# A selective scan whose input term for two of four states is made by ScalarE and TensorE: prediction and result

## The chip, the cores and the metric

The kernel runs on one core of a Trainium2 chip. A core has five engines with a queue of instructions each: TensorE (PE; its weight loads are listed apart as PEld), VectorE (DVE), ScalarE (ACT), GpSimd (POOL) and SyncE (SP), which here only starts DMAs. Each engine works through its queue in order; an instruction whose input or buffer isn't ready holds up all that stands behind it on the same engine. The metric is the device time of one launch in microseconds. The kernel before took 32,186.01 us (median of three runs, 32,183.83 to 32,190.26).

## The reference

Two layers on an image of 256 x 256 tokens with 128 channels, each with a group norm ahead and added to its input. Layer 0 is attention along rows. Layer 1, where the change lies, is a two-dimensional selective scan (four scan directions, 256 inner channels, 16 states per channel). Cut to what matters:

```python
delta = softplus(dts + dt_bias)                      # per token and channel
def step(h, inp):                                    # over 65,536 tokens
    d_t, x_t, B_t, C_t = inp
    dA = exp(d_t[..., None] * As)                    # channel x state
    h = dA * h + (d_t * x_t)[..., None] * B_t        # the input term is B * delta * x
    y = einsum('bkdn,bkn->bkd', h, C_t)              # sum over the 16 states
    return h, y
```

x_dbl = xs @ x_proj_w gives the 8 rows from which dts comes, and B and C of 16 rows each. The four directions' results are added, normalised, multiplied by a gate and projected.

## The kernel before, in words

The front part (both group norms, the attention, the input projection and the 3 x 3 convolution) ends at about 5,536 us of the profile and isn't touched. All the rest is the scan stage, from line 635 on.

**Tiling.** Each direction (order 2, 1, 3, 0) goes through 65,536 tokens in 128 chunks of T = 512 tokens: 512 chunks in all, numbered q. A chunk has NG = 8 steps g, one for each 32 of the 256 channels. A step has NI = 4 iterations n; each handles one state index i for all 32 channels, with four states j side by side: 4 x 32 = 128 partitions by 512 tokens. "Slot" means one such iteration, numbered 4g + n, 32 to a chunk. In a slot, in this order:

- ScalarE makes dA = exp(A * delta) from dr, the delta of 32 channels repeated over four states (line 1122). Some slots have an evacuation of sums (`evacuate`) here.
- One piece each of the generators that are due is emitted: `turn`, those in `later` (`store` or `finish` of a chunk that is done), `prepare`, and some of `products`.
- VectorE runs the scan h = dA * h + input along the 512 tokens (line 1148), with the last h of the chunk before from hst.

**The input term B * delta * x.** du = delta * x is made once per chunk. For three states i < NB = 3, TensorE spreads du over the four states into the PSUM tile ur (`spread_du`, line 864), and VectorE multiplies ur by B_r (`times_B`, line 875, 128 x 1536) into bx, in which the scans then run in place. For the fourth state, TensorE turns du to tokens x channels (`turn`, line 816), ScalarE copies it to duT (line 822) and multiplies by B, which is a number per token there (`products`, line 834: 32 ACTIVATEs of 128 x 128 per chunk), and TensorE turns the result back into the PSUM tile bl (`turn_back`, line 846, four transposes per step), from which the scan reads. One ur buffer and one bl buffer are there, three PSUM buffers for dA, two in SBUF for dAl (the dA of the fourth state), and two PSUM buffers "mm" that all other work shares.

**Behind the scans.** GpSimd copies the last h to hst (line 1167) and multiplies the four scanned states by C (line 1168). `sums` (line 890) adds up the states by TensorE products with a 0/1 matrix, 16 for each half of the channels: those of steps 0 to 3 are emitted at slots 23 and 24, those of steps 4 to 7 at slot 4 of the next chunk.

**Preparation of chunk q + 2** starts at slot 21 (g = 5, n = 1) with a piece per slot: transposes of the tokens (tps), copies to xs, the projection pb and its copy bc (line 747), the dt product pv, and then softplus as max(v, 0) + log1p(exp(-|v|)), with a correction of log1p's rounding: Abs, Relu, Exp, two Identity, Ln on ScalarE, and a subtraction and two additions on GpSimd. delta goes to memory and comes back spread (`spread_delta`, dr). `until(now, then)` is a row of empty pieces, which sets how many slots lie between two pieces.

**What sets the order.** `manual_schedule`: each engine gets its instructions in the order in which the Python code emits them. Buffers and data alone set the waits.

Of the kernel before, what the change touches and what calls it, by code (L numbers as in the profile page):

```python
# [16 lines left out]
P = 128  # L17
# [49 lines left out]
def attention_and_scan_kernel(  # L67
# [568 lines left out]
    NI = 4  # L636
    NB = 3
    sw = ctx.enter_context(tc.tile_pool(name="sw", bufs=1))
# [36 lines left out]
    for q in range(4):  # L675
# [3 lines left out]
        )  # L679
    neg_one = sw.tile([P, 1], F32, name="neg_one")  # L680
    nc.vector.memset(neg_one, -1.0)
    hst = sw.tile([P, NG, NI], F32, name="hst")
# [38 lines left out]
    def prepare(q):  # L721
# [5 lines left out]
        for h in range(2):  # L727
# [6 lines left out]
            yield  # L734
        yield from until(2, 5)
        for h, tp in enumerate(tps):
# [3 lines left out]
        for h in range(2):  # L740
            nc.tensor.matmul(  # L741
                pb, xw_in[:, k, h, :], xs[:, h, :], start=(h == 0), stop=(h == 1)
            )
        yield
        yield
        bc = io.tile([R + 2 * NS, T], F32, name="bc", bufs=1)
# [3 lines left out]
        yield  # L750


        e = io.tile([P, 2, T], F32, name="e", bufs=1)
# [21 lines left out]
        C_r = io.tile([P, NI, T], F32, name="C_r")  # L775
        for m, t, ni in ((0, B_r, NB), (1, C_r, NI)):
# [6 lines left out]
        yield  # L783
        lg = io.tile([P, 2, T], F32, name="lg", bufs=1)
        nc.scalar.activation(lg, e, AF.Identity, bias=1.0)
        yield
        du = io.tile([P, 2, T], F32, name="du")
        nc.scalar.activation(du, lg, AF.Identity, bias=neg_one)
        B_t = io.tile([P, 4, R + 2 * NS], F32, name="B_t")
        nc.scalar.copy(B_t, tp)  # L790
        yield
        nc.gpsimd.tensor_tensor(e, e, du, ALU.subtract)  # L792
        yield
        yield
        nc.scalar.activation(lg, lg, AF.Ln)  # L795
        yield
        nc.gpsimd.tensor_tensor(lg, lg, e, ALU.add)  # L797
        yield
        nc.gpsimd.tensor_tensor(delta, delta, lg, ALU.add)  # L799
        de_d = sd.tile([DI, T], F32, name="de_d")  # L800
        nc.sync.dma_start(de_d.rearrange("(h p) t -> p h t", p=P), delta)
        yield
        nc.gpsimd.tensor_tensor(du, delta, xs, ALU.mult)  # L803
        prepared[q] = xs, de_d, du, B_r, C_r, B_t

    def turn(q):

        duT = io.tile([P, 4, DI], F32, name="duT", bufs=1)
        turned[q] = duT
        tps = []  # L810
        for w in range(2):
            tp = sps.tile([P, 2, DI], F32, name="tpd", tag="mm")
            for b in range(2):
                for h in range(2):
                    t0 = (2 * w + b) * P
                    nc.tensor.transpose(
                        tp[:, b, h * P : (h + 1) * P], prepared[q][2][:, h, t0 : t0 + P], ident
                    )
            tps.append(tp)
        yield  # L820
        for w, tp in enumerate(tps):
            nc.scalar.copy(duT[:, 2 * w : 2 * w + 2, :], tp)
            yield

    def products(q, h):


        bt = wk.tile([P, 4, 4, 4, 32], F32, name=f"bt{h}", bufs=1)
        products_of[q, h] = bt
        duT, B_t = turned[q], prepared[q][5]  # L830
        for b in range(4):
            for j in range(4):
                n = R + NI * j + NB
                nc.scalar.mul(  # L834
                    bt[:, b, :, j, :],
                    duT[:, b, h * P : (h + 1) * P].rearrange("t (g c) -> t g c", c=32),
                    B_t[:, b, n : n + 1],
                )
                yield

    def turn_back(q, g):

        bl = sps.tile([P, T], F32, name="bl", bufs=1)
        bt = products_of[q, g // 4]
        for b in range(4):
# [4 lines left out]

    def spread_delta(q, h):

        de_d = prepared[q][1]
        dr = io.tile([P, 4, T], F32, name="dr")
        for j in range(4):
            nc.sync.dma_start(
                dr[32 * j : 32 * j + 32],
                de_d[h * P : (h + 1) * P, :].rearrange("(q c) t -> c q t", c=32),
            )
        return dr  # L860
# [86 lines left out]
    def finish(q, yos):  # L947
# [50 lines left out]
        for h in range(2):  # L998
# [86 lines left out]
    drain(preparing)  # L1085
    preparing.append(products(0, 0))
    drain(preparing)
# [3 lines left out]
    preparing.append(prepare(1))  # L1091
    for _ in range(2 * NI + 3):
        piece(preparing)
    begin_sums(0, 0)
    turning, multiplying, summing = [], [], []
    bls = {(0, 0): turn_back(0, 0)}
    multiplying.append(products(0, 1))
    for _ in range(4):
        piece(multiplying)


    counts = {1: [0, 0, 2, 2], 3: [2, 2, 2, 2], 5: [0, 0, 3, 3], 6: [2, 2, 2, 2], 7: [2, 2, 2, 0]}
    for s, (q, g) in enumerate(all_steps):
        k, a = steps[q]
        nxt = all_steps[s + 1] if s + 1 < len(all_steps) else None
        if g == 1:
            drs[q, 1] = spread_delta(q, 1)
# [4 lines left out]
        if g == 5 and q + 1 < NQ:  # L1112
            drain(preparing)
            drs[q + 1, 0] = spread_delta(q + 1, 0)
        dr = drs[q, g // 4][:, g % 4, :]
        hs = bxs.pop((q, g))
        for n, i in enumerate((NB, *range(NB))):
            if i < NB:
                dA = sps.tile([P, T], F32, name="dA", bufs=3)
            else:  # L1120
# [27 lines left out]
            nc.vector.tensor_tensor_scan(  # L1148
                hs[:, i, :],
                dA,  # L1150
                hs[:, i, :] if i < NB else bls.pop((q, g)),
                0.0 if a == 0 else hst[:, g, i : i + 1],
# [12 lines left out]
        if g % 4 == 3:  # L1165
            del drs[q, g // 4]
        nc.gpsimd.tensor_copy(hst[:, g, :], hs[:, :, T - 1])  # L1167
        nc.gpsimd.tensor_tensor(hs, hs, prepared[q][4], ALU.mult)  # L1168
        hcs[q, g] = hs
    drain([sums(NQ - 1, 1)])  # L1170
    summed[NQ - 1] = load_sum(NQ - 1)
# [62 lines left out]
```

## Time and profile before

| | |
|---|---|
| median of the runs | 32,186.01 us |
| the profiled execution, its span | 32,185.1 us |
| scan stage, from its first product at 5,576 us | 26,609 us |
| one chunk in directions 2, 1, 3 (distance of products at the same step) | 51.20 us |
| one chunk in direction 0, the last | 53.85 us (mean) |
| first product to last product of the four directions | 5,576 / 12,139 / 18,690 / 25,241 to 32,126 us |
| mean granted TensorE clock | 0.853 |

Busy times are unions over an engine's instructions. Two instructions in a row on one engine overlap at their ends, so the duration of one is longer than its share of the queue; the distance between the starts of two instructions that stand back to back is what one costs. In brackets behind an instruction of a timeline stands the idle time ahead of it, and what ended that.

### The profile page before, as it was taken

How to read it: one execution, taken by the hardware profiler on the slowest of the kernel's cores; microseconds unless marked ns; L12 is line 12 of the kernel's file. 1: busy time of each engine (PE TensorE's matmuls, PEld its weight loads, DVE VectorE, ACT ScalarE, POOL GpSimd, SP SyncE). 2: the span in 40 equal slices, each digit the busy share in tenths (PEclk: the TensorE clock that was granted, in tenths of full speed). 3: DMA queues.
4: the chain of work that ended last, by engine and by line, in shares of the span. 5: the costliest groups of instructions: out<-in, count | busy, mean ns of one | idle time of the engine just before them, and what ended most of it. 6: DMA issues, size and time to landing. Idle time of an engine off the chain costs nothing.

```text
span 32185.1 us, 380702 instructions
## 1 busy us (share of the span) xinstructions
PE 23853.4 (74%) x122902; PEld 10868.3 (34%) x122902; DVE 29575.2 (92%) x29023; ACT 25201.0 (78%) x50438; POOL 25710.4 (80%) x11291
## 2 busy tenths in 40 slices
PE   6999988666676667777777777777777777777777
PEld 3555544222222222222222232223222333333333
DVE  7666633999999999999999999999999999999999
ACT  5555522888888888888888888888888888888888
POOL 4222200999999999999999999999999999999998
PEclk9999999888888888888888888888888888888888
DMA  4001033444444444444444444444444555555554
GB/s 143 30 28 29 27 105 121 110 109 108 111 109 108 110 110 118 119 121 120 119 120 122 119 119 121 121 119 119 122 119 118 123 124 124 123 123 123 124 123 113
DMA packets 2100469, 3518.55 MB, mean 109 GB/s; under 512 B 201112, under 2 KB 1187096, under 8 KB 2022560
## 3 DMA queue, kind: packets, MB, share of 16 engines
q1 hardware_dynamic: 2093296, 3476.09, 43.3%
q8 instruction: 967, 15.84, 0.2%
q10 hardware_dynamic: 5168, 18.12, 0.1%
q14 instruction: 1038, 8.50, 0.1%
HBM read 2754.18 MB, written 739.25 MB: 109 GB/s over the span
## 4 chain that ended last, share of the span: by engine, by line
PE 32%; ACT 24%; DVE 22%; issue 12%; POOL 9%; DMA 2%; SPq 0%; ACTq 0%; POOLq 0%; DVEq 0%
DVE bx L1148 11%; PE yp L890 8%; DVE bx L875 7%; ACT dA L1122 6%; PE ur L864 6%; POOL bx L1168 5%; PE pb L741 3%; ACT bt L834 2%; PE pc L563 2%; ACT dAl L1122 2%; PE av L393 2%; PE tpy L913 2%; POOL at L370 2%; ACT e L765 2%; ACT L795 2%
## 5 line engine op out<-in xcount | busy, mean ns | idle before, releaser
L1168 POOL TENSOR_TENSOR bx<-bx,C_r 128x2048 f32<-128x2048 f32 x4096 | 18604.4, 4542 | 334.3 <-POOL hst L1167 5.8
L1148 DVE TENSOR_TENSOR_SCAN bx<-dA,hst,bx 128x512 f32<-128x512 f32 x12192 | 15074.4, 1264 | 217.2 <-ACT dA L1122 215.3
L1122 ACT ACTIVATE dA<-dr,A_s 128x512 f32<-128x512 f32 x12288 | 8329.3, 683 | 2247.5 <-DVE bx L1148 2199.6
L864 PE MATMUL ur<-du,spread 128*128 128x512 f32 x8192 | 5710.1, 787 | 4498.5 <-DVE bx L875 4378.8
L875 DVE TENSOR_TENSOR bx<-B_r,ur 128x1536 f32<-128x1536 f32 x4096 | 7075.5, 1727 | 40.1 <-DMA dr<-de_d 40.1
L834 ACT ACTIVATE bt<-duT,B_t 128x128 f32<-128x128 f32 x16384 | 5572.5, 392 | 698.7 <-PE bl L846 698.7
L1148 DVE TENSOR_TENSOR_SCAN bx<-dAl,hst,bl 128x512 f32<-128x512 f32 x4064 | 5096.6, 1254 | 24.2 <-PE bl L846 24.1
L890 PE MATMUL yp<-bx,gather 128*32 128x512 f32 x32768 | 5052.5, 771 | 7.5 <-POOL bx L1168 6.4
L846 PE MATMUL bl<-ident,bt 128*128 128x128 f32 x16384 | 2714.8, 289 | 2441.0 <-DVE bx L1148 2439.0
L846 PEld LDWEIGHTS bl<-ident,bt 128*128 128x128 f32 x16384 | 1791.0, 143 | 4323.4 <-DVE bx L1148 3240.7
L864 PEld LDWEIGHTS ur<-du,spread 128*128 128x128 f32 x8192 | 1451.2, 223 | 5027.9 <-DVE bx L875 5023.9
L370 POOL TENSOR_TENSOR at<-at,sm 128x2048 f32<-128x2048 f32 x256 | 922.2, 3603 | 2719.7 <-DVE sm L369 2550.6
L1122 ACT ACTIVATE dAl<-dr,A_s 128x512 f32<-128x512 f32 x4096 | 2919.2, 713 | 0.0
L890 PEld LDWEIGHTS yp<-bx,gather 128*32 128x32 f32 x32768 | 1165.1, 139 | 4348.3 <-issue 3834.9
L1167 POOL COPY hst<-bx 128x4 f32<-128x4 f32 x4096 | 771.4, 188 | 1615.5 <-DVE bx L1148 1588.6
L362 ACT ACTIVATE at<-at,mx 128x256 f32<-128x256 f32 x2048 | 1016.1, 498 | 472.5 <-DVE mx L358 468.1
L792 POOL TENSOR_TENSOR e<-e,du 128x1024 f32<-128x1024 f32 x512 | 1202.8, 2349 | 138.3 <-DMA C_r<-bc_d 138.3
L799 POOL TENSOR_TENSOR delta<-delta,lg 128x1024 f32<-128x1024 f32 x512 | 1209.9, 2363 | 40.1
L803 POOL TENSOR_TENSOR du<-delta,xs 128x1024 f32<-128x1024 f32 x512 | 1205.4, 2354 | 40.2
L758 PE MATMUL pv<-bc,dtw_s 8*128 8x512 f32 x2048 | 1019.6, 616 | 256.5 <-ACT bc L747 256.5
L797 POOL TENSOR_TENSOR lg<-lg,e 128x1024 f32<-128x1024 f32 x512 | 1205.0, 2354 | 0.2 <-ACT lg L795 0.2
L391 DVE COPY aT<-atp 128x512 f32<-128x512 f32 x512 | 353.6, 691 | 774.8 <-PE atp L382 771.0
(173 smaller groups left out, 31933.7 us busy)
## 6 DMA issues: line engine op xcount, KB each, us to landing
dr<-de_d SPq DMA_DIRECT2D x4096, 256.0 KB
C_r<-bc_d SPq DMA_DIRECT2D x2048, 256.0 KB
B_r<-bc_d SPq DMA_DIRECT2D x2048, 192.0 KB
de_d<-delta SPq DMA_DIRECT2D x512, 512.0 KB
xtok<-xc_d SPq DMA_DIRECT2D x256, 512.0 KB
xtok<-xc_d SPq DMA_DIRECT2D x512, 256.0 KB
yl<-y_d SPq DMA_DIRECT2D x512, 256.0 KB
y_d<-yt SPq DMA_DIRECT2D x512, 256.0 KB
```

Source lines behind the costliest of these rows:

```text
L370: nc.gpsimd.tensor_tensor(at, at, sm.unsqueeze(3).to_broadcast([P, H, 2, S]), ALU.mult,)
L797: nc.gpsimd.tensor_tensor(lg, lg, e, ALU.add)
L799: nc.gpsimd.tensor_tensor(delta, delta, lg, ALU.add)
L803: nc.gpsimd.tensor_tensor(du, delta, xs, ALU.mult)
L834: nc.scalar.mul(bt[:, b, :, j, :], duT[:, b, h * P : (h + 1) * P].rearrange("t (g c) -> t g c", c=32), B_t[:, b, n : n + 1],)
L846: nc.tensor.transpose(bl[:, b * P : (b + 1) * P], bt[:, b, g % 4].rearrange("t j c -> t (j c)"), ident)
L864: nc.tensor.matmul(ur, spread[:, g % 4].rearrange("p j c -> p (j c)"), prepared[q][2][:, g // 4, :], start=True, stop=True,)
L875: nc.vector.tensor_tensor(bx[:, :NB, :], prepared[q][3], ur.unsqueeze(1).to_broadcast([P, NB, T]), ALU.mult,)
L890: nc.tensor.matmul(yp[32 * g : 32 * g + 32, :], gather, hc[:, i, :], start=(i == 0 and steps[q][0] != ORDER[0]), stop=True, skip_group_che ...
L1122: nc.scalar.activation(dA, dr, AF.Exp, scale=A_s[:, k, g // 4, g % 4, i : i + 1])
L1148: nc.vector.tensor_tensor_scan(hs[:, i, :], dA, hs[:, i, :] if i < NB else bls.pop((q, g)), 0.0 if a == 0 else hst[:, g, i : i + 1], ALU.mult,
L1168: nc.gpsimd.tensor_tensor(hs, hs, prepared[q][4], ALU.mult)
```

## The change

NB goes from 3 to 2: the input term of two states, not one, is made on tokens by ScalarE and turned back by TensorE. So `times_B` covers 128 x 1024, `products` makes 64 multiplications per chunk (two tiles bt per half of the channels), and `turn_back` is called twice per step, with two bl buffers; the dA buffers in PSUM go from three to two. The order of states within a step alternates (2, 0, 3, 1). Softplus is one ScalarE function on the two halves of pv, and the arithmetic around it on ScalarE and GpSimd goes. dr is loaded for two steps at a time, two steps ahead. duT has two buffers. The loads of B_r and C_r stand under the last `until` of `prepare`, the four transposes of du ahead of each copy in `turn`, and in `products` each of the two tiles gets 16 multiplications with a piece each. The pieces of `prepare`, `turn` and `finish` are placed anew, and two `products` pieces are emitted in every slot.

```diff
-    NB = 3
+    NB = 2
+    SHARE = 0
-    neg_one = sw.tile([P, 1], F32, name="neg_one")
-    nc.vector.memset(neg_one, -1.0)
 def prepare(q):
-        yield from until(2, 5)
+        yield from until(2, 3)
         for h, tp in enumerate(tps):
             nc.scalar.copy(xs[:, h, ::-1] if k >= 2 else xs[:, h, :], tp)
             yield
...
-        yield
-        yield
+        yield from until(5, 7)
         bc = io.tile([R + 2 * NS, T], F32, name="bc", bufs=1)
         nc.scalar.copy(bc, pb)
...
+        yield from until(8, 10)
+        for h, pv in enumerate(pvs):
+            nc.scalar.activation(
+                delta[:, h, :], pv, AF.Softplus, bias=dtb_s[:, k, h : h + 1]
+            )
+        de_d = sd.tile([DI, T], F32, name="de_d")
+        nc.sync.dma_start(de_d.rearrange("(h p) t -> p h t", p=P), delta)
         yield
-        yield
-        for h, pv in enumerate(pvs):
-            nc.scalar.activation(e[:, h, :], pv, AF.Abs, bias=dtb_s[:, k, h : h + 1])
-            nc.scalar.activation(delta[:, h, :], pv, AF.Relu, bias=dtb_s[:, k, h : h + 1])
-            yield
         tp = sps.tile([P, 4, R + 2 * NS], F32, name="tpb", tag="mm")
...
-        nc.scalar.activation(e, e, AF.Exp, scale=-1.0)
+        yield from until(11, 13)
+        du = io.tile([P, 2, T], F32, name="du")
+        nc.gpsimd.tensor_tensor(du, delta, xs, ALU.mult)
+        B_t = io.tile([P, 4, R + 2 * NS], F32, name="B_t")
+        nc.scalar.copy(B_t, tp)
...
+        yield from until(13, 20)
         for m, t, ni in ((0, B_r, NB), (1, C_r, NI)):
...
-        nc.scalar.activation(lg, e, AF.Identity, bias=1.0)
-        nc.scalar.activation(du, lg, AF.Identity, bias=neg_one)
-        nc.gpsimd.tensor_tensor(e, e, du, ALU.subtract)
-        nc.scalar.activation(lg, lg, AF.Ln)
-        nc.gpsimd.tensor_tensor(lg, lg, e, ALU.add)
-        nc.gpsimd.tensor_tensor(delta, delta, lg, ALU.add)
 def turn(q):
-        duT = io.tile([P, 4, DI], F32, name="duT", bufs=1)
+        duT = io.tile([P, 4, DI], F32, name="duT")
         for w in range(2):
...
+            yield
+            nc.scalar.copy(duT[:, 2 * w : 2 * w + 2, :], tp)
 def products(q, h):
+        bts = [wk.tile([P, 4, 4, 4, 32], F32, name=f"bt{h}{i}", bufs=1) for i in range(NI - NB)]
+        for i, bt in enumerate(bts):
...
-def turn_back(q, g):
+def turn_back(q, g, i):
+        bl = sps.tile([P, T], F32, name=f"bl{i}", bufs=1)
-def spread_delta(q, h):
+def spread_delta(q, g):
-        dr = io.tile([P, 4, T], F32, name="dr")
+        dr = io.tile([P, 2, T], F32, name="dr")
 def finish(q, yos):
-        for j, now, then in ((0, 15, 16), (1, 16, 19), (2, 19, 20), (3, 20, 27)):
+        for j, now, then in ((0, 15, 16), (1, 16, 19), (2, 19, 20), (3, 20, 23)):
-        yield from until(27, 31)
+        yield from until(23, 25)
...
-        yield from until(33, 36)
+        yield from until(27, 28)
...
-        yield from until(36, 40)
+        yield from until(28, 30)
...
-        yield from until(40, 55)
+        yield from until(30, 39)
...
-        yield from until(55, 58)
+        yield from until(39, 41)
...
-    preparing.append(products(0, 0))
+    preparing.extend([products(0, 0), products(0, 1)])
-    counts = {1: [0, 0, 2, 2], 3: [2, 2, 2, 2], 5: [0, 0, 3, 3], 6: [2, 2, 2, 2], 7: [2, 2, 2, 0]}
+    PER = 2
+        if g % 2 == 0 and s + 2 < len(all_steps):
+            drs[all_steps[s + 2]] = spread_delta(*all_steps[s + 2])
-        for n, i in enumerate((NB, *range(NB))):
+        for n, i in enumerate((NB, 0, NB + 1, 1)):
             if i < NB:
-                dA = sps.tile([P, T], F32, name="dA", bufs=3)
+                dA = sps.tile([P, T], F32, name="dA", bufs=2)
-            if g == 4 and n == 3 and q + 1 < NQ:
+            if n == 3 and g == 1 and q + 1 < NQ:
                 turning.append(turn(q + 1))
-            if g == 5 and n == 2 and q + 1 < NQ:
+            if n == 0 and g == 3 and q + 1 < NQ:
                 multiplying.append(products(q + 1, 0))
-            if g == 7 and n == 1 and q + 1 < NQ:
+            if n == 0 and g == 7 and q + 1 < NQ:
                 multiplying.append(products(q + 1, 1))
             if g == 5 and n == 1 and q + 2 < NQ:
                 preparing.append(prepare(q + 2))
-            for _ in range(counts[g][n] if g in counts else 0):
+            for _ in range(PER):
                 piece(multiplying)
...
             if n == 1 and nxt:
                 bxs[nxt] = times_B(nxt[0], urs.pop(nxt))
-            if n == 3 and nxt:
-                bls[nxt] = turn_back(*nxt)
+            if n % 2 and nxt:
+                bls[(*nxt, n // 2)] = turn_back(*nxt, n // 2)
             if n == 3 and s + 2 < len(all_steps):
                 urs[all_steps[s + 2]] = spread_du(*all_steps[s + 2])
```

More of the change, by code (lines that the diff above doesn't have):

```diff
@@ L750, in prepare @@
         yield
-        e = io.tile([P, 2, T], F32, name="e", bufs=1)
         delta = io.tile([P, 2, T], F32, name="delta", bufs=1)
@@ L772, in prepare @@
             )
-        nc.scalar.activation(e, e, AF.Exp, scale=-1.0)
+        yield from until(11, 13)
[3 more added lines that the diff above has]
+        nc.scalar.copy(B_t, tp)
         B_r = io.tile([P, NB, T], F32, name="B_r")
         C_r = io.tile([P, NI, T], F32, name="C_r")
+        prepared[q] = xs, de_d, du, B_r, C_r, B_t
+        yield from until(13, 20)
         for m, t, ni in ((0, B_r, NB), (1, C_r, NI)):
@@ L782, in prepare @@
                 )
-        yield
-        lg = io.tile([P, 2, T], F32, name="lg", bufs=1)
-        nc.scalar.activation(lg, e, AF.Identity, bias=1.0)
-        yield
-        du = io.tile([P, 2, T], F32, name="du")
-        nc.scalar.activation(du, lg, AF.Identity, bias=neg_one)
-        B_t = io.tile([P, 4, R + 2 * NS], F32, name="B_t")
-        nc.scalar.copy(B_t, tp)
-        yield
-        nc.gpsimd.tensor_tensor(e, e, du, ALU.subtract)
[L793 to L796, printed above, removed]
-        nc.gpsimd.tensor_tensor(lg, lg, e, ALU.add)
-        yield
-        nc.gpsimd.tensor_tensor(delta, delta, lg, ALU.add)
[L800 to L804, printed above, removed]
     def turn(q):
-        duT = io.tile([P, 4, DI], F32, name="duT", bufs=1)
+        duT = io.tile([P, 4, DI], F32, name="duT")
         turned[q] = duT
-        tps = []
         for w in range(2):
@@ L818, in turn @@
                     )
-            tps.append(tp)
+            yield
+            nc.scalar.copy(duT[:, 2 * w : 2 * w + 2, :], tp)
         yield
-        for w, tp in enumerate(tps):
-            nc.scalar.copy(duT[:, 2 * w : 2 * w + 2, :], tp)
-            yield
     def products(q, h):
-        bt = wk.tile([P, 4, 4, 4, 32], F32, name=f"bt{h}", bufs=1)
-        products_of[q, h] = bt
+        bts = [wk.tile([P, 4, 4, 4, 32], F32, name=f"bt{h}{i}", bufs=1) for i in range(NI - NB)]
+        products_of[q, h] = bts
         duT, B_t = turned[q], prepared[q][5]
[L831 to L839, printed above, removed]
-    def turn_back(q, g):
-        bl = sps.tile([P, T], F32, name="bl", bufs=1)
-        bt = products_of[q, g // 4]
+        for i, bt in enumerate(bts):
+            for b in range(4):
+                for j in range(4):
+                    n = R + NI * j + NB + i
+                    to = bt[:, b, :, j, :]
+                    of = duT[:, b, h * P : (h + 1) * P].rearrange("t (g c) -> t g c", c=32)
+                    by = B_t[:, b, n : n + 1]
+                    if SHARE and (4 * b + j) % SHARE == SHARE - 1:
+                        nc.gpsimd.tensor_scalar(to, of, by, None, ALU.mult)
+                    else:
+                        nc.scalar.mul(to, of, by)
+                    yield
+    def turn_back(q, g, i):
+        bl = sps.tile([P, T], F32, name=f"bl{i}", bufs=1)
+        bt = products_of[q, g // 4][i]
         for b in range(4):
@@ L857, in spread_delta @@
                 dr[32 * j : 32 * j + 32],
-                de_d[h * P : (h + 1) * P, :].rearrange("(q c) t -> c q t", c=32),
+                de_d[32 * g : 32 * g + 64, :].rearrange("(q c) t -> c q t", c=32),
             )
@@ L1091, in attention_and_scan_kernel @@
     preparing.append(prepare(1))
-    for _ in range(2 * NI + 3):
-        piece(preparing)
+    drain(preparing)
     begin_sums(0, 0)
     turning, multiplying, summing = [], [], []
[L1096 to L1099, printed above, removed]
-    counts = {1: [0, 0, 2, 2], 3: [2, 2, 2, 2], 5: [0, 0, 3, 3], 6: [2, 2, 2, 2], 7: [2, 2, 2, 0]}
+    bls = {(0, 0, i): turn_back(0, 0, i) for i in range(NI - NB)}
+    PER = 2
     for s, (q, g) in enumerate(all_steps):
@@ L1105, in attention_and_scan_kernel @@
         nxt = all_steps[s + 1] if s + 1 < len(all_steps) else None
-        if g == 1:
-            drs[q, 1] = spread_delta(q, 1)
+        if g % 2 == 0 and s + 2 < len(all_steps):
+            drs[all_steps[s + 2]] = spread_delta(*all_steps[s + 2])
         if g == 2 and q and steps[q - 1][0] != ORDER[0]:
@@ L1111, in attention_and_scan_kernel @@
             load(q + 2)
[L1112 to L1115, printed above, removed]
+        dr = drs[q, g - g % 2][:, g % 2, :]
         hs = bxs.pop((q, g))
-        for n, i in enumerate((NB, *range(NB))):
+        for n, i in enumerate((NB, 0, NB + 1, 1)):
             if i < NB:
-                dA = sps.tile([P, T], F32, name="dA", bufs=3)
+                dA = sps.tile([P, T], F32, name="dA", bufs=2)
             else:
@@ L1150, in attention_and_scan_kernel @@
                 dA,
-                hs[:, i, :] if i < NB else bls.pop((q, g)),
+                hs[:, i, :] if i < NB else bls.pop((q, g, i - NB)),
                 0.0 if a == 0 else hst[:, g, i : i + 1],
@@ L1164, in attention_and_scan_kernel @@
                 piece(summing)
-        if g % 4 == 3:
-            del drs[q, g // 4]
         nc.gpsimd.tensor_copy(hst[:, g, :], hs[:, :, T - 1])
@@ L1169, in attention_and_scan_kernel @@
         hcs[q, g] = hs
+        if g % 2:
+            del drs[q, g - 1]
     drain([sums(NQ - 1, 1)])
```

## The prediction

> **What bounds the kernel now.** I read the page's busy shares and costliest groups first, then the busy time of one whole chunk, then the timelines of VectorE, ScalarE and TensorE in that chunk. A slot is one pass of the inner loop, numbered 4g + n within a chunk (32 slots, four to a step).
>
> ```profile
> PE 23853.4 (74%) x122902; PEld 10868.3 (34%) x122902; DVE 29575.2 (92%) x29023; ACT 25201.0 (78%) x50438; POOL 25710.4 (80%) x11291
> ...
> L875 DVE TENSOR_TENSOR bx<-B_r,ur 128x1536 f32<-128x1536 f32 x4096 | 7075.5, 1727 | 40.1 <-DMA dr<-de_d 40.1
> L834 ACT ACTIVATE bt<-duT,B_t 128x128 f32<-128x128 f32 x16384 | 5572.5, 392 | 698.7 <-PE bl L846 698.7
> ```
>
> ```profile
> 20005.40:20056.60 51.20, 36.27 (x160) 15.03 (x160) 50.99 (x41) 43.43 (x85) 46.85 (x20) 0.83 0.48 120
> ```
>
> The columns of the second line are window, length, busy PE, PEld, DVE, ACT, POOL, granted clock, DMA share, GB/s. In one chunk VectorE is busy 50.99 of 51.20 us: it is the bound. ScalarE has 7.8 us free, TensorE 14.9, GpSimd 4.4.
>
> ```profile
> 20011.06 1.73 DVE L875 TENSOR_TENSOR bx<-B_r,ur 128x1536 f32<-128x1536 f32 x1
> 20012.70 2.45 DVE L1148 TENSOR_TENSOR_SCAN bx<-dA,hst,bx 128x512 f32<-128x512 f32 x2
> 20015.07 1.25 DVE L1148 TENSOR_TENSOR_SCAN bx<-dAl,hst,bl 128x512 f32<-128x512 f32 x1
> 20016.24 1.26 DVE L1148 TENSOR_TENSOR_SCAN bx<-dA,hst,bx 128x512 f32<-128x512 f32 x1
> 20017.42 1.73 DVE L875 TENSOR_TENSOR bx<-B_r,ur 128x1536 f32<-128x1536 f32 x1
> ```
>
> Instructions overlap, so I cost by distance of starts: the product takes 1.64 us, a scan 1.18, a step 6.36.
>
> ```profile
> 20003.41 0.97 ACT L834 ACTIVATE bt<-duT,B_t 128x128 f32<-128x128 f32 x3
> 20004.29 0.71 ACT L1122 ACTIVATE dAl<-dr,A_s 128x512 f32<-128x512 f32 x1
> 20004.90 0.68 ACT L834 ACTIVATE bt<-duT,B_t 128x128 f32<-128x128 f32 x2
> ...
> 20017.33 0.58 ACT L747 COPY bc<-pb 40x512 f32<-40x512 f32 x1 [0.91 <-PE pb L741]
> ...
> 20031.22 1.28 ACT L795 ACT_TABLE_LOAD   x1
> 20032.52 1.06 ACT L795 ACTIVATE lg<-lg 128x1024 f32<-128x1024 f32 x1
> 20033.59 1.28 ACT L1122 ACT_TABLE_LOAD   x1
> ```
>
> A bt costs 0.295 us (0.88 for three), an Exp 0.61, a load 1.30. ScalarE already waits for TensorE at bc; that is harmless now because it runs ahead of VectorE.
>
> ```profile
> 20006.48 2.08 PE L864 MATMUL ur<-du,spread 128*128 128x512 f32 x2 [2.16 <-DVE bx L875]
> 20008.48 5.52 PE L890 MATMUL yp<-bx,gather 128*32 128x512 f32 x32
> 20013.93 0.66 PE L846 MATMUL bl<-ident,bt 128*128 128x128 f32 x4
> 20014.42 1.02 PE L864 MATMUL ur<-du,spread 128*128 128x512 f32 x2
> 20015.38 1.91 PE L741 MATMUL pb<-xs,xw_in 128*40 128x512 f32 x4
> ...
> 20025.56 1.70 PE L864 MATMUL ur<-du,spread 128*128 128x512 f32 x2 [2.16 <-DVE bx L875]
> 20027.19 4.70 PE L890 MATMUL yp<-bx,gather 128*32 128x512 f32 x32
> ```
>
> Twice a chunk 16 gather products (32 records) go to TensorE in one burst: 5.45 us or 4.64, by start distance. bl of step 7 comes out behind the first burst at 20013.93 + 0.66 = 20014.59, and its scan starts at 20015.07: 0.5 us to spare.
>
> **The sums, part by part.**
>
> VectorE: the product covers 1024 elements, not 1536. Two thirds of 1.64 us is 1.10; I take 1.11. Step 4 x 1.18 + 1.11 = 5.83, chunk 46.6 (now 50.9): 4.3 us less.
>
> ScalarE: 32 more bt x 0.295 = +9.4. Removed: Abs and Relu 4 x 0.57, Exp and Identity (128x1024) 0.95 each, Identity with a bias tile 1.04, Ln 1.07: -6.3. Softplus is in no row; its nearest is Abs on the same tile, 0.57 (between a copy's 0.48 and 0.67 for gz): two make 1.1. The two loads per chunk stay if Softplus, like Ln, isn't loaded together with Exp; the ends are no load (-2.7) and four (+2.6). I take two. Net +4.3, so ScalarE needs 43.4 + 4.3 = 47.7 us. Counted from starts alone: 32 x (0.61 + 0.59) = 38.5 and 8.4 for the rest = 46.9. It now needs as long as VectorE. Per slot it has 1.46 - 1.20 = 0.25 us to gain on it.
>
> The price per state shows in these rows: VectorE gives up 0.53 us a step, ScalarE takes four bt, 1.18 us, and TensorE four transposes, 0.49.
> [...]
>
> TensorE: 32 more transposes at about 0.165 = +5.2, 41.5 us. GpSimd: three of 2.35 us go, 46.9 - 7.1 = 39.8; du stays. Cover for both is the longer chunk.
>
> SP: 16 issues of dr per chunk, not 8 (0.46 us each, 1.85 for four), half as large; B_r and C_r move to slot 9 of the next chunk, behind dr, yl and xtok, about 3 MB in step 2. At the 209 GB/s that the busiest stretch of this chunk shows (share 1.02) that is 14.4 us, and dr for step 6 is issued 12 us after them and read 12 us after that: hidden. If not, ScalarE stands at step 6 for the rest. de_d goes out earlier, at slot 31, ahead of two chunks' slack. The prologue makes 48 more bt: +14 us. The two set-up instructions for neg_one are nothing.
>
> Order is where it costs. Two bl and one ur buffer: bl of state 2 is refilled in slot n = 1, that of state 3 at n = 3, ahead of ur. So TensorE in step 5 waits until scan 22 has read the second bl, 1.18 us later than now, and issues four transposes before ur and the burst. pb moves from slot 28 to 26, bc from 30 to 28.
>
> The dA buffers go from three to two, like dAl's: ScalarE can be four slots (5.8 us) ahead at most. duT's second buffer removes a wait that the trace doesn't list; nothing is counted for it.
>
> *Stretch A*, from the end of scan 22, with the cheaper burst (1.63 + 4.64) and handoffs of 0.05: transposes 0.05 to 0.55; ur to 2.18; burst to 6.82; bl for step 7 to 7.31, ready 7.48; pb 7.31 to 9.22. Scan 28 would start at 5 x 1.18 + 1.11 = 7.01: it waits to 7.5. ScalarE stands at bc until 9.27, though about 2 us ahead. Then bc 0.48, two bt 0.59, dA29 0.69: scan 29 starts at 11.05, not 8.19. Its lead is gone. dA30 starts 11.54, yo comes between, dA31 13.22; from 13.83 a load (1.44 with its wait), two Softplus 1.2, two bt 0.59, a load 1.30, so dA32 is ready at 19.1. Scan 32 would start at 12.84: 6.3 us lost.
>
> *Stretch B*, from the end of scan 2: the burst drained at slot 4 ends at 6.82, bl at 7.31; the first du transposes of turn are ready at 7.97. ScalarE, 2.0 us ahead by then (8 x 0.25), stands at duT until 8.02; copy 0.48, bt 0.59, dA9 0.69: scan 9 at 9.8, not 8.19: 1.6 lost. A further 0.2 goes at slot 12, where yo falls.
>
> Chunk: 46.6 + 6.3 + 1.6 + 0.2 = 54.7 us, now 51.2. With the dearer burst (ur 2.0, burst 5.45: 1.18 more in each stretch) 57.1. With TensorE at full clock throughout (ur 0.95, the burst eight rounds of 0.43 = 3.44, 1.88 less) A loses 4.4 and B nothing: 51.1. I take the cheaper burst, because TensorE will be somewhat busier ahead of it.
>
> The clock: matmuls of 512 columns take 0.59 us in the stretch with a granted clock of 1.00 and 1.06 where it is 0.51; both bursts begin slow behind 2.16 us of waiting. After the change 2.4 us of waiting for scan 22 remain ahead of the burst, so it begins slow again.
> [...]
>
> The last direction (128 chunks) has 1.57 us of VectorE statistics, two yn at slots 31 and 32 (0.49 each) and part of gz (2 x 0.67, less the lead of 0.85): +2.9, so 57.6. Moving finish closer gains nothing else; it lies beside the waits.
>
> Total: 5576 to the first product, 14, 384 x 54.7 = 21,005, 128 x 57.6 = 7,373, and 55 behind the last step: 34,023. The same sum for now, 5576 + 384 x 51.2 + 128 x 53.85 + 55 = 32,185, is the profiled execution's span of 32,185.1; the median of the runs shown is 32,186.0, so I carry nothing over. Predicted: 34,020.
>
> **Rivals.**
> 1. *Faster:* ScalarE never really waits for TensorE and both engines run near full. For it: neither's own sum passes 47.7. Against: pb and bl stand behind a burst in TensorE's order. It decides if the path from scan 22 to bc is under about 5.5 us instead of 9.3. Chunk 47.3, last direction 50.9: 5645 + 18,163 + 6,515 = 30,320.
> 2. *Level:* TensorE stays at full clock, chunk 51.1 and 54.0: 5645 + 19,622 + 6,912 = 32,180. Against: the idle time before the bursts.
> 3. *Dearer burst, or extra loads:* 57.1 and 60.0 give 35,250; four loads give 34,020 + 512 x 2.6 = 35,350.
> 4. *No load for Softplus:* 34,020 - 512 x 2.7 = 32,640. Against: Ln costs two.
>
> **How the numbers follow.** Likeliest 0.62 (33,400 to 35,000), rival 1 0.15, rival 2 0.08 (of it 0.03 faster, 0.03 same, 0.02 slower), rival 3 0.09, rival 4 0.06. A measurement tells about 0.2%, 64 us. Faster 0.18, same 0.03, slower 0.79. The range leaves out rival 1 and what lies above 35,300: 32,150 to 35,300, for the likeliest case alone 33,400 to 35,000.
>
> **What would show it.** VectorE under 0.90 busy in the scan, waiting for ScalarE's dA mostly; ScalarE waiting for pb at bc (some 2 to 5 us a chunk) and for tpd at duT; the wait for scans down from 2083 us; the product at about 1.2 us mean, x4096; two loads per chunk. I am wrong if bc finds pb ready, or if VectorE stays above 0.97 busy.

## The result and the profile after

The changed kernel takes 33,548.5 us (median of four runs, 33,523 to 33,571) against 32,184.9 us: a ratio of 1.0425, 95% interval 1.0412 to 1.0437. The forecast was 34,020 us. The profiled execution spans 33,558.9 us; the figures per chunk below come from distances between the products `times_B` in that trace. Where nothing else is said they are means: in the first three directions the distance from a direction's first product to the next direction's, over 128 chunks, in the last the mean distance of products at the same step. The directions run in the order 2, 1, 3, 0; 1 and 3 are called the middle ones.

The busy shares and the groups of the changed kernel's page, in the columns of before (line, engine, instruction, count, busy us, mean ns, idle before with its main releaser):

```profile
PE 25097.2 (75%) x139286; PEld 13094.5 (39%) x139286; DVE 27574.9 (82%) x29022; ACT 27076.5 (81%) x63747; POOL 22258.1 (66%) x9755
...
L819 ACT ACTIVATE bt<-duT,B_t 128x128 f32<-128x128 f32 x32768 | 11294.2, 396 | 4.3 <-PE bl L827 4.3
...
L856 DVE TENSOR_TENSOR bx<-B_r,ur 128x1024 f32<-128x1024 f32 x4096 | 4896.8, 1196 | 51.7 <-PE ur L845 48.3
...
L745 ACT COPY bc<-pb 40x512 f32<-40x512 f32 x512 | 297.8, 582 | 1959.1 <-PE pb L740 1959.1
L800 ACT COPY duT<-tpd 128x512 f32<-128x512 f32 x1024 | 598.9, 585 | 1268.9 <-PE tpd L796 1268.9
```

The product did become cheaper, 1,196 ns for 1,727: 2,179 us of busy time over 4,096 of them. And ScalarE now waits 1,959 us for pb and 1,269 us for the transposes of du; before, the trace had 455 us and 9 us for these two. VectorE went from 92% to 82% busy. No engine is busy for nine tenths of the time any more.

One chunk of direction 3 (window, length, busy PE, PEld, DVE, ACT, POOL, granted clock, DMA share, GB/s):

```profile
20002.90:20057.50 54.60, 39.27 (x192) 19.59 (x192) 47.12 (x41) 46.99 (x111) 40.10 (x18) 0.81 0.40 108
```

VectorE needs 47.1 us and ScalarE 47.0 us, in a chunk of 54.6. 7.5 us are waits of both. Stretch A of the prediction, from the end of scan 22 at about 20,002.9, on TensorE:

```profile
20002.97 1.08 PE L827 MATMUL bl<-ident,bt 128*128 128x128 f32 x4 [2.48 <-DVE bx L1122]
20003.85 1.91 PE L845 MATMUL ur<-du,spread 128*128 128x512 f32 x2
20005.69 3.94 PE L871 MATMUL yp<-bx,gather 128*32 128x512 f32 x32
20009.56 0.66 PE L827 MATMUL bl<-ident,bt 128*128 128x128 f32 x4
20010.15 1.91 PE L740 MATMUL pb<-xs,xw_in 128*40 128x512 f32 x4
```

on ScalarE:

```profile
20006.71 0.73 ACT L1096 ACTIVATE dAl<-dr,A_s 128x512 f32<-128x512 f32 x1
20012.10 0.58 ACT L745 COPY bc<-pb 40x512 f32<-40x512 f32 x1 [4.65 <-PE pb L740]
...
20016.74 1.28 ACT L759 ACT_TABLE_LOAD   x1
20018.03 1.26 ACT L759 ACTIVATE delta<-pv,dtb_s 128x512 f32<-128x512 f32 x2
...
20019.89 1.28 ACT L1096 ACT_TABLE_LOAD   x1
20021.19 0.72 ACT L1096 ACTIVATE dAl<-dr,A_s 128x512 f32<-128x512 f32 x1
```

and on VectorE:

```profile
20010.33 1.28 DVE L1122 TENSOR_TENSOR_SCAN bx<-dAl,hst,bl 128x512 f32<-128x512 f32 x1 [0.51 <-PE bl L827]
20013.88 1.28 DVE L1122 TENSOR_TENSOR_SCAN bx<-dA,hst,bx 128x512 f32<-128x512 f32 x1 [2.28 <-ACT dA L1096]
...
20021.94 1.28 DVE L1122 TENSOR_TENSOR_SCAN bx<-dAl,hst,bl 128x512 f32<-128x512 f32 x1 [3.30 <-ACT dAl L1096]
```

Read the three together. TensorE can't refill bl for step 6 before scan 22 has read it, so ur, the burst of sums, bl for step 7 and pb all come late. ScalarE has made dA28 and stands at bc for 4.65 us. Scan 28 waits 0.51 us for bl. Scan 29 waits 2.28 us for a dA that ScalarE could only begin behind bc. Then, with no lead left, the two loads and Softplus make scan 32 wait 3.30 us. Counted from 20,002.9, bc starts after 9.2 us, scan 29 after 11.0, scan 32 after 19.0.

### The profile page after: what moved, and what is told of

Its sections match the earlier page's. It is cut to its first block, busy times and chain, and to the rows that moved or that the text cites. A ratio compares the mean times of both kernels' runs of the same rounds, so it can differ in the third digit from the quotient of the medians.

```text
span 33558.9 us, 434075 instructions
## 1 busy us (share of the span) xinstructions
PE 25097.2 (75%) x139286; PEld 13094.5 (39%) x139286; DVE 27574.9 (82%) x29022; ACT 27076.5 (81%) x63747; POOL 22258.1 (66%) x9755
## 4 chain that ended last, share of the span: by engine, by line
ACT 37%; PE 32%; DVE 14%; issue 6%; DMA 6%; SPq 2%; POOL 2%; ACTq 0%; POOLq 0%; DVEq 0%
ACT bt L819 14%; PE yp L871 10%; DVE bx L1122 9%; ACT dA L1096 7%; ACT dAl L1096 6%; PE ur L845 4%; PE bl L827 4%; DMA B_r<-bc_d 3%; PE pb L740 3%; DVE bx L856 2%; ACT L1096 2%; PE pc L563 2%; ACT L759 2%; PE av L393 2%; POOL at L370 2%
## 5 line engine op out<-in xcount | busy, mean ns | idle before, releaser
L1122 DVE TENSOR_TENSOR_SCAN bx<-dAl,hst,bl 128x512 f32<-128x512 f32 x8128 | 10301.3, 1267 | 2206.3 <-ACT dAl L1096 1740.1
L827 PE MATMUL bl<-ident,bt 128*128 128x128 f32 x32768 | 6047.2, 315 | 7586.9 <-DVE bx L1122 7586.4
L1122 DVE TENSOR_TENSOR_SCAN bx<-dA,hst,bx 128x512 f32<-128x512 f32 x8128 | 10246.1, 1261 | 1361.2 <-ACT dA L1096 1361.2
L819 ACT ACTIVATE bt<-duT,B_t 128x128 f32<-128x128 f32 x32768 | 11294.2, 396 | 4.3 <-PE bl L827 4.3
L827 PEld LDWEIGHTS bl<-ident,bt 128*128 128x128 f32 x32768 | 4123.5, 158 | 10472.5 <-issue 6746.0
L1096 ACT ACTIVATE dAl<-dr,A_s 128x512 f32<-128x512 f32 x8192 | 5858.1, 715 | 17.8 <-DVE bx L1122 7.8
L1096 ACT ACTIVATE dA<-dr,A_s 128x512 f32<-128x512 f32 x8192 | 5563.1, 679 | 3.1 <-DVE bx L1122 3.1
L856 DVE TENSOR_TENSOR bx<-B_r,ur 128x1024 f32<-128x1024 f32 x4096 | 4896.8, 1196 | 51.7 <-PE ur L845 48.3
L871 PE MATMUL yp<-bx,gather 128*32 128x512 f32 x32768 | 4053.9, 637 | 7.3 <-POOL bx L1140 7.3
L800 ACT COPY duT<-tpd 128x512 f32<-128x512 f32 x1024 | 598.9, 585 | 1268.9 <-PE tpd L796 1268.9
```

Of the source, the lines that this page charges most:

```text
L819: nc.scalar.mul(to, of, by)
L827: nc.tensor.transpose(bl[:, b * P : (b + 1) * P], bt[:, b, g % 4].rearrange("t j c -> t (j c)"), ident)
L856: nc.vector.tensor_tensor(bx[:, :NB, :], prepared[q][3], ur.unsqueeze(1).to_broadcast([P, NB, T]), ALU.mult,)
L871: nc.tensor.matmul(yp[32 * g : 32 * g + 32, :], gather, hc[:, i, :], start=(i == 0 and steps[q][0] != ORDER[0]), stop=True, skip_group_che ...
L1096: nc.scalar.activation(dA, dr, AF.Exp, scale=A_s[:, k, g // 4, g % 4, i : i + 1])
L1122: nc.vector.tensor_tensor_scan(hs[:, i, :], dA, hs[:, i, :] if i < NB else bls.pop((q, g, i - NB)), 0.0 if a == 0 else hst[:, g, i : i + 1 ...
```

## The experiments

Two readings of the loss were tried against each other, with a third beside them. *Order*: the two engines' work fits, but pb, bl and du's transposes stand behind a burst in TensorE's queue, and ScalarE, whose lead is small now, stands behind them. *Capacity*: 64 multiplications per chunk are more than ScalarE can do in the time. *Clock*: the bursts cost what they cost because TensorE's clock is down when they begin (the two of the chunk above start at 20,005.69 and 20,029.57 us, where the granted clock is 0.5, and take 3.94 and 3.95 us).

**The burst split.**

```diff
-            if n == 0 and g == 1 and q:
-                drain([sums(q - 1, 1)])
-            if n == 0 and g == 6:
-                drain(summing)
...
             piece(preparing)
+            if n == 2 and g == 1 and q:
+                summing.append(sums(q - 1, 1))
+            if n == 2 and g == 5:
+                summing.append(sums(q, 0))
+            if n == 2 and g in (1, 2, 5, 6):
+                piece(summing)
+                piece(summing)
...
-            if n == 3 and g == 5:
-                summing.append(sums(q, 0))
-                piece(summing)
```

> The 16 sums of each half are emitted as two pairs of four products in two steps, at n = 2 behind the first bl of a step, and no longer as one burst. ScalarE's and VectorE's work is as in the changed kernel. Theory 'order' (bl, pb and du's transposes stand behind a burst in TensorE's queue, and ScalarE behind them): ScalarE's waits at bc and duT nearly go, the stretch from scan 22 to bc takes 5 to 6.5 us instead of 9.2, a chunk 48 to 50 us instead of 54.6, the whole 30,700 to 31,700 us. Rival 'capacity' (ScalarE simply has too much to do with 64 multiplications per chunk): unchanged at about 33,550, since no work leaves ScalarE. Rival 'clock' (bursts run slow because TensorE's clock is down when they begin): the halves begin slow as well, 33,000 or more.

Measured: 31,281.3 us, ratio to before 0.972 (0.969 to 0.975). No work was taken from any engine. A chunk takes 49.3 us in the first three directions. Its busy times and two lines of its waits (engine and line, waited for, us in total, times, longest):

```profile
20003.00:20052.00 49.00, 37.89 (x192) 19.06 (x188) 47.04 (x42) 47.35 (x111) 40.50 (x18) 0.86 0.43 121
```

```profile
ACT duT L800 <- PE tpd L796: 650.5, 414, 2.5
...
ACT bc L745 <- PE pb L740: 186.9, 389, 0.7
```

VectorE's and ScalarE's busy times are those of the changed kernel, 47.0 and 47.4, but the chunk is 5 us shorter. The wait for pb is nearly gone: from the end of scan 22 to the start of bc it is 4.9 us (median in direction 1), counted in the same way 9.3 in the changed kernel. Order holds; capacity, which had 33,550, falls as the cause of the 54.6 us. It comes back later as a floor: ScalarE is busy for 47.4 of 49.0. The granted clock rose as well, from 0.81 to 0.86, so a part of the 5 us may be the clock's; a run below has a price for that.

**Half of the multiplications left out.** The tile of the second state stays zero, so its part of the input term is missing.

```diff
+    still = [sw.tile([P, 4, 4, 4, 32], F32, name=f"still{h}") for h in range(2)]
+    for t in still:
+        nc.vector.memset(t, 0.0)
...
-        bts = [wk.tile([P, 4, 4, 4, 32], F32, name=f"bt{h}{i}", bufs=1) for i in range(NI - NB)]
+        bts = [wk.tile([P, 4, 4, 4, 32], F32, name=f"bt{h}0", bufs=1), still[h]]
...
-        for i, bt in enumerate(bts):
+        for i, bt in enumerate(bts[:1]):
...
-    PER = 2
+    PER = 1
```

> The 32 multiplications per chunk of the second of the two states are left out (its tile stays zero; TensorE still turns it back, the scans still run), one piece per slot instead of two: ScalarE has 9.4 us less per chunk, 38.3 us. Rival 'capacity': VectorE alone bounds, 46.6 to 47.5 us a chunk, about 30,000 in all. Theory 'order': ScalarE still waits for pb and duT, longer than before since it arrives earlier, and then has 0.6 us less to do per slot: scan 29 still 2.6 us late, scan 32 some 5 in all instead of 6.3, scan 9 1.3: about 53 us a chunk, 32,700 to 33,000 in all.

Measured: 32,758.2 us, ratio 1.018 (1.015 to 1.021), 52.3 us a chunk in directions 1 and 3. ScalarE was freed of a fifth of its work and the kernel is still slower than before:

```profile
ACT bc L748 <- PE pb L743: 2422.7, 482, 6.8
ACT duT L803 <- PE tpd L799: 2420.7, 962, 6.1
```

The freed time went into longer waits for the same two things. This is the plainest evidence against capacity.

**TensorE kept busy ahead of the bursts.**

```diff
+        again = 3 if (g, i) in ((5, 0), (5, 1), (6, 0), (0, 0), (0, 1), (1, 0)) else 1
-        for b in range(4):
+        for b in [b for _ in range(again) for b in range(4)]:
             nc.tensor.transpose(
```

> The transposes of six of the sixteen bl of a chunk, in the steps ahead of the two bursts, are made three times over, so that TensorE is busy ahead of the bursts. The result is the same. If the clock is then up when a burst begins, bl, ur and the burst take 4.9 us instead of 6.6 in each of the two stretches. Theory 'clock': a chunk 51 to 52 us, the whole about 32,260. Theory 'order' with the clock as a part of its price: the same saving if the clock is up, and 54 us or more if the added transposes only make the queue longer. Rival 'capacity': 33,550 either way.

Measured: 32,816.0 us, ratio 1.020 (1.017 to 1.023), between the two figures. In directions 1 and 3 most chunks (76 of 127 in each, by the products of step 7) take 51.4 us and the rest 53.6 or 55.0. Stretch A's burst is fast in all of them, stretch B's in those of 51.4 us only. Stretch A, in a chunk where both take 3.64 us:

```profile
20068.15 0.63 PE L828 MATMUL bl<-ident,bt 128*128 128x128 f32 x4 [1.28 <-DVE bx L1123]
20068.61 1.02 PE L846 MATMUL ur<-du,spread 128*128 128x512 f32 x2
20069.57 3.64 PE L872 MATMUL yp<-bx,gather 128*32 128x512 f32 x32
20073.14 0.66 PE L828 MATMUL bl<-ident,bt 128*128 128x128 f32 x4
```

From the first line to the last the burst's path takes 4.99 us, not 6.59. In the changed kernel's trace all 333 bursts that start at a granted clock of 1.0 take 3.64 us, and the 689 that start at 0.5 take 3.95 (median). The mean granted clock is 0.934 in this run and 0.854 in the changed kernel. So the clock is a part of the price, about 3 us a chunk where both bursts run fast, and 48 useless transposes more per chunk made the kernel 2% faster than without them. It isn't the whole: 51.4 us is no better than before, and splitting the burst is worth 2 us more.

**No table load.** Relu stands for Softplus, so the softplus is left out. In the kernel before Relu takes 0.68 us on the same tile, at 20,020.81 and 20,022.56 us, with no load next to it.

```diff
-                delta[:, h, :], pv, AF.Softplus, bias=dtb_s[:, k, h : h + 1]
+                delta[:, h, :], pv, AF.Relu, bias=dtb_s[:, k, h : h + 1]
```

> Relu takes the place of Softplus, so that ScalarE needs no table load in the scan stage; delta is max(v, 0) alone, and the softplus is left out. ScalarE loses 2.7 us per chunk. Theory 'order': the wait of scan 32 goes from 3.3 us to about 0.6, those at scans 9 and 29 stay, 51.9 us a chunk, 32,170 in all. Rival 'capacity': ScalarE's 47.7 us fall to 45, under VectorE's 46.6, so a chunk takes about 47 us and the whole about 30,000.

Measured: 31,853.4 us, ratio 0.990 (0.987 to 0.993). The chunk comes to 51.20 us, not 51.9: 1,695 us less, where 2.7 us a chunk make 1,380. Capacity's 30,000 is far off. In the middle directions the step of scan 32 goes from 9.23 to 6.43 us: 2.8 us for the two loads, as predicted. The other two steps with waits, which the expectation had left as they were, move too. That of scan 29 goes from 8.82 to 7.22 us, because stretch A's burst is now fast (ur and burst take 1.02 and 3.64 us from 20,012.93 on, not 1.91 and 3.94, and bc starts 7.7 us after scan 22, not 9.3; the mean granted clock is 0.91); that of scan 9 goes from 7.43 to 8.43, because stretch B's burst is slower (4.9 us, not 3.95). The balance is the 0.6 to 0.7 us a chunk more.

**One copy more per chunk.**

```diff
+    pad_a = sw.tile([P, 256], F32, name="pad_a")
+    pad_b = sw.tile([P, 256], F32, name="pad_b")
+    nc.vector.memset(pad_a, 0.0)
...
+            if n == 0 and g == 4:
+                nc.vector.tensor_copy(pad_b, pad_a)
             nc.vector.tensor_tensor_scan(
```

> The changed kernel with one more VectorE copy (128x256, some 0.2 to 0.35 us) per chunk at slot 16, where VectorE sets the pace. If the chunk is held to a whole number of the clock's windows (54.61 us is 16 of 3.413), it is taken up: 54.61 us in directions 1 and 3 as before, the whole within 50 us of 33,550. If the chunk is just the sum of its parts: 0.2 to 0.35 us more per chunk, 33,650 to 33,730.

Measured: 33,633.5 us, 85 us above the changed kernel's median; 33,606.3 against 33,558.9 by the profiled spans. The copy takes 0.27 us by itself and lengthens step 4 by 0.21 us (5.82 to 6.03). Yet directions 1 and 3 still take 54.61 us a chunk (medians; means 54.61 with the copy, 54.60 and 54.59 without): there it is taken up. The step with scan 29 is 0.13 us shorter (8.82 to 8.69) and that with scan 9 by 0.07 (7.43 to 7.36). Direction 2, the first, goes from 53.63 to 54.12, and the last from 55.58 to 55.39. So each chunk is held to a fixed length in the two middle directions and not in the others. What the traces show of the expectation's windows is that the records of the granted clock are whole multiples of 3.413 us long (last section). The total lies between the expectation's two ranges; neither allowed for both kinds at once.

**One part alone: Softplus in the kernel before.**

```diff
-            nc.scalar.activation(e[:, h, :], pv, AF.Abs, bias=dtb_s[:, k, h : h + 1])
-            nc.scalar.activation(delta[:, h, :], pv, AF.Relu, bias=dtb_s[:, k, h : h + 1])
+            nc.scalar.activation(
+                delta[:, h, :], pv, AF.Softplus, bias=dtb_s[:, k, h : h + 1]
+            )
...
-        nc.scalar.activation(e, e, AF.Exp, scale=-1.0)
-        nc.scalar.activation(lg, e, AF.Identity, bias=1.0)
-        nc.scalar.activation(du, lg, AF.Identity, bias=neg_one)
-        nc.gpsimd.tensor_tensor(e, e, du, ALU.subtract)
-        nc.scalar.activation(lg, lg, AF.Ln)
-        nc.gpsimd.tensor_tensor(lg, lg, e, ALU.add)
-        nc.gpsimd.tensor_tensor(delta, delta, lg, ALU.add)
```

> The kernel before with one part of the change alone: Softplus as one function (the Abs, Relu, Exp, two Identity and Ln and GpSimd's three operations go, every piece stays in its slot, three states stay on VectorE). ScalarE loses some 5 us and GpSimd 7 us per chunk, but VectorE bounds at 51.2. Theory 'order' and the rival 'capacity' both: no change to 0.3 us per chunk less, 32,030 to 32,190 us. If Softplus were itself the cause of the loss (more table loads than Ln): 2.6 us per chunk more, 33,500.

Measured: 31,964.0 us, ratio 0.993 (0.991 to 0.995). Softplus is not the cause of the loss; it is a gain of its own, a little larger than expected. The chunk is 50.89 us (median), eight steps of 6.36 and nothing else: the 0.31 us that one step lost behind Ln's loads is gone. The last direction went from 53.85 to 52.82, which the expectation had left out.

**duT's copies three slots behind their transposes**, on top of the split burst.

```diff
+        tps = []
...
-            yield
-            nc.scalar.copy(duT[:, 2 * w : 2 * w + 2, :], tp)
-        yield
+            tps.append(tp)
+            yield
+        yield from until(2, 3)
+        for w, tp in enumerate(tps):
+            nc.scalar.copy(duT[:, 2 * w : 2 * w + 2, :], tp)
+            yield
```

> The split sums of the first experiment, and duT's two copies three slots behind the transposes that they read (slots 10 and 11), no longer one. With the split sums alone ScalarE still waited 651 us in all for these transposes. Theory 'order': that wait goes, some 1.0 us a chunk, 30,700 to 30,900 us. From here ScalarE's own 47.6 us per chunk is the floor: by it alone 5645 + 384 x 47.6 + 128 x 51.2 = 30,480, so nothing below that.

Measured: 31,133.3 us, ratio 0.967 (0.966 to 0.969): 148 us less than with the split alone, not the 400 to 600 expected. The wait at duT is gone from the list, but the one at bc rose from 187 to 515 us: ScalarE arrives earlier at the next thing that isn't ready.

**Every eighth multiplication to GpSimd**, on top of that: `SHARE = 8`.

> As the run with the copies moved, and every eighth of the 64 multiplications per chunk goes to GpSimd. ScalarE loses 8 x 0.295 = 2.4 us per chunk and comes below VectorE's 46.6. If ScalarE is the limit by then: 0.8 to 2 us a chunk less than without it, 29,900 to 30,500 us. If the limit is the one wait behind the table loads, which comes whatever ScalarE's average is: 30,600 to 30,900. What GpSimd takes for one is in no row; above some 0.9 us it would itself become late.

Measured: 30,877.4 us, ratio 0.959 (0.958 to 0.961).

```profile
L821 POOL TENSOR_SCALAR bt<-duT,B_t 128x128 f32<-128x128 f32 x4096 | 2484.7, 607 | 2.1 <-ACT duT L804 2.1
```

GpSimd takes 607 ns for one, ScalarE 394 in the same run. The chunk goes from 48.84 to 48.46 us: the second of the two expectations. The scan at the start of a chunk still came 1.7 us late behind the loads.

**Three pieces one slot later**, and then **po two slots earlier, with its copy four slots behind it.**

```diff
-        yield from until(5, 7)
+        yield from until(5, 8)
         bc = io.tile([R + 2 * NS, T], F32, name="bc", bufs=1)
...
-            if n == 0 and g == 3 and q:
+            if n == 1 and g == 3 and q:
                 evacuate(q - 1, 1)
...
-            if n == 3 and g == 1 and q + 1 < NQ:
+            if n == 0 and g == 2 and q + 1 < NQ:
                 turning.append(turn(q + 1))
```

> As the run with every eighth multiplication on GpSimd, and three pieces one slot later: bc (and with it pv, Softplus and B_t), the start of turn, and the evacuation of the second half's sums. In that run ScalarE still waited 686 us in all at bc and 354 us at yo, some 2 us a chunk, and then came 1.8 us late to the first scan of a chunk behind the table loads. Theory 'order': these waits shrink to under 1 us a chunk, and as much of the wait behind the loads with them: 47.2 to 48.0 us a chunk, 30,200 to 30,600 us in all. If the wait behind the loads is set by the block of loads and Softplus alone (3.9 us, more than ScalarE can be ahead): unchanged, 30,850.

Measured: 30,934.1 us, ratio 0.961 (0.960 to 0.963), no gain in all. The first three directions came to 47.8 to 47.9 us, as expected. The last went from 51.64 to 54.34: `finish` had moved by a slot as well, and ScalarE now stood 635 us at xo for po, where it had stood 353. That was not foreseen. It is the same pattern, a copy two slots behind its TensorE work.

```diff
+        xr = io.tile([P, 4, D], F32, name="xr", bufs=1)
+        nc.sync.dma_start(xr, x2_d[a : a + T, :].rearrange("(j p) c -> p j c", p=P))
         yn = io.tile([P, 4, DI], F32, name="yn", tag="yl", bufs=1)
...
-        xr = io.tile([P, 4, D], F32, name="xr", bufs=1)
-        nc.sync.dma_start(xr, x2_d[a : a + T, :].rearrange("(j p) c -> p j c", p=P))
-        yield from until(30, 39)
+        yield from until(30, 37)
         po = sps.tile([P, 4, D], F32, name="po", tag="mm")
...
-        yield from until(39, 41)
+        yield from until(37, 41)
         xo = io.tile([P, 4, D], F32, name="xo", tag="xr", bufs=1)
```

> As the run with three pieces one slot later, and in the last direction the projection po two slots earlier (slot 18), its copy xo four slots behind it, no longer two, with the load xr ahead of both. In that run the first three directions came to 47.8 us a chunk, but in the last one ScalarE waited 635 us in all at xo for po, some 5 us in each of the 128 chunks, and the chunk took 54.3 us. Theory 'order': this is the same thing as bc behind pb. The wait goes, the last direction comes to 50.5 to 51.5 us a chunk, 30,450 to 30,600 us in all, under the 30,877 of the best run so far. If the last direction is bound by ScalarE's work there (some 3.7 us more per chunk): 52 us or more, 30,650 and above.

Measured: 30,369.4 us, ratio 0.943 (0.942 to 0.945): 5.7% faster than before, and 9.5% faster than the change as it stood. The last direction takes 49.95 us a chunk, less than was expected, and so does the whole. What ScalarE and VectorE still wait for:

```profile
DVE bx L1129 <- ACT dA L1100: 549.0, 492, 1.3
ACT dAl L1100 <- DVE bx L1129: 266.0, 478, 1.0
...
ACT bc L745 <- PE pb L740: 183.6, 364, 0.5
```

VectorE's wait for dA is down to 1.1 us a chunk (549.0 over 492), and ScalarE waits for VectorE again now and then, as it did before the change. All the runs built on the split kernel have two dA buffers, so going from three to two isn't what held the chunk at 54.6 us. No run gives the kernel before the same order of work, but VectorE with three states needs 8 x 6.36 = 50.9 us a chunk whatever the order; this run's chunks take 47.8 us in the middle directions.

## Why the prediction was right, and where it was off

*VectorE.* 5.83 us a step was predicted; every undisturbed step takes 5.82.

*ScalarE.* 47.7 or 46.9 us per chunk by two ways of counting; 46.99. Two loads per chunk, as Ln had (1,283 ns each in the mean, 511 ahead of Softplus and 511 behind it); two Softplus take 1.16 us by their starts, against 1.1. The end with no load was 1,380 us below the forecast; taking the loads away gave 1,695 below the changed kernel.

*Stretch A.* bc at 9.27, scan 28 at 7.5, scan 29 at 11.05 and scan 32 at 19.1 us were walked by hand; 9.2, 7.4, 11.0 and 19.0 are in the trace. The loss of 6.3 us is there. The parts inside are less exact: the slow bl takes 0.88 us and not 0.5, ur 1.84 and not 1.63, the burst 3.87 and not 4.64; that they cancel (6.59 us in all against 6.77) is luck.

*Stretch B.* Scan 9 was to be 1.6 us late. At 20,036.37 it starts 9.7 us after the end of scan 2 (predicted 9.8), and that step takes 7.43 us, not 5.82. The 0.2 us at slot 12 isn't there: no scan of that chunk waits behind yo.

*The chunk.* 54.7 predicted, 54.60 and 54.59 in the middle directions. The mechanism is the predicted one. That the number comes so near is in part luck: the parts of the burst's path cancel, and, as the run with one copy more shows, the chunk is held at 54.61 us against small differences.

*The signs.* All that were named are there: VectorE is busy for 0.86 of the chunk, ScalarE waits 3.8 us a chunk at bc (1,959 us over 512) and stands at duT, its wait for scans has gone from 2,083 to 11 us, the product takes 1,196 ns, and there are two loads per chunk.

*What failed.* The term for the last direction: 57.6 predicted, 55.58 measured, 258 us over 128 chunks. (Its three additions come to 3.0 us, not 2.9.) The finish's work did cost what was added for it: against the middle directions the step of scan 32 is 1.01 us longer (10.24 for 9.23) and that of the statistics 1.81 (7.63 for 5.82), 2.8 us in all. But the losses of the two stretches are smaller there, in the mean by 0.91 us in the step of scan 29 (7.91 for 8.82) and by 0.94 in that of scan 9 (6.49 for 7.43). The step that failed is that the bursts begin slow in every chunk. In the chunk from 29,982 on, both run at a granted clock of 1.00 (from 29,992.45 to 29,997.04 and from 30,016.63 to 30,020.21 us); stretch A:

```profile
29991.98 0.63 PE L827 MATMUL bl<-ident,bt 128*128 128x128 f32 x4 [2.48 <-DVE bx L1122]
29992.45 1.02 PE L845 MATMUL ur<-du,spread 128*128 128x512 f32 x2
29993.40 3.64 PE L871 MATMUL yp<-bx,gather 128*32 128x512 f32 x32
```

The wait ahead of it is the 2.48 us of the chunk shown before, where ur and burst took 1.91 and 3.94. So the 2.4 us of waiting, from which the prediction concluded that the burst begins slow, doesn't settle it alone. The first direction was mis-sized for the same reason, 53.63 instead of 54.7: 137 us. There stretch A's burst takes 3.6 us in all of the 120 chunks from the sixth on, bc starts 7.7 us after scan 22 and not 9.3, and the step of scan 29 takes 7.22 us; only the step of scan 9 is 0.5 us longer (7.90 for 7.43). The mean granted clock is 0.85 in the first and the last direction and 0.81 in the middle ones. TensorE has the work of po and tpz ahead of the bursts in the last direction; that can't be the whole reason, since the first has neither, and what sets the clock at a burst's start stays open. With 27 us from the middle directions and 25 at the start these make up 447 of the 464 us between 34,023 and the span.

*The rivals.* The faster one needed a path from scan 22 to bc under about 5.5 us; it is 9.2, and when the split burst brought it to 4.9 the kernel did become faster than before. The full clock's 51.1 us a chunk was nearly reached, at 51.4, by the run that kept TensorE busy, whose granted clock was 0.934 in the mean. Softplus's loads stayed at two.

*The multiplications.* The change as it stood lost 4.25%, but not because of the multiplications themselves: with half of them left out the kernel was still 1.8% slower than before. With the same split of the four states, less an eighth of ScalarE's multiplications on GpSimd, the last run is 5.7% under the kernel before and 5.0% under that kernel with Softplus alone (30,369 against 31,964). And that though ScalarE takes 1.18 us a step for what VectorE did in 0.53: here it mattered how full each engine was (before, VectorE 92% and ScalarE 78%), and in what order the work stood.

## What to carry to other kernels

When work moves from a full engine to one that was merely less full, the lead of the second goes: waits for a third engine that cost nothing while it ran ahead are then paid in full (here ScalarE's at bc, 455 us before and 1,959 after). Before such a move, look through the queue of the third for a burst that stands ahead of something small that others wait for, split it, and put each copy of its results several slots behind the work it reads, in every stage (here bc, duT and xo in turn). A walk by hand through one period, with start distances from the trace, gave the middle directions' chunk to within 0.2 us; adding up busy times gave a gain where there was a loss.

## What the runs showed of the hardware that was not expected

In many of the runs the chunk takes whole multiples of one length. In the middle directions it is 51.20 us before (15 x 3.413), 54.61 after (16 x 3.413), 54.61 with a 0.27 us copy added, 51.20 with Relu for Softplus (medians). In the changed kernel's trace the granted clock is 0.5 or 1.0 in each of its 3,048 records. In one chunk it changes at 20,002.94, 20,006.36, 20,016.60, 20,030.25, 20,040.49, 20,043.90 and 20,057.56 us: all distances are multiples of 3.413 us, and the pattern repeats with the chunk. The length of every record but the last is a multiple of 3,413.3 ns to within 2 ns.

Where a single chunk is no multiple, a group of chunks that repeats often is. In the changed kernel's first direction 53.62, 54.11 and 52.70 us come round again and again, together 160.43 us, 47 x 3.413. With TensorE kept busy, directions 1 and 3 repeat five chunks of 262.83 us (77 x 3.413); with half of the multiplications, three chunks of 157.01 us (46 x 3.413). It isn't so in every run: with Softplus alone in the kernel before, where VectorE hardly ever waits, 126 of the first direction's 127 distances are 50.9 us, 14.9 times the length.

Why a chunk keeps to such a length was not shown. Shown is that a 0.27 us piece of work vanished in the two middle directions, and that a saving of 2.8 us became 3.4, as stretch A's burst came down to 3.64 us and stretch B's went up to 4.9. So this kernel, whose loop passes through two slow bursts, hid a small change and magnified a larger one. With the burst split, single chunks of 49.1, 48.7 and 48.4 us (medians) are no multiples; the 47.79 us of the last two runs' first direction is one again, the fourteenth.
